# Key-weight squares on another engine, four heads' scores in one PSUM bank, and a new table of wanted times in a decoder kernel

## The chip, the cores and the metric

The kernel runs on one core of a Trainium2 chip. The core has a matrix engine (PE, TensorE), a vector engine (DVE), a scalar engine (ACT), a general engine (POOL, GpSimd) and a queue that issues its DMA transfers (SP). Each engine works through its own list of instructions in the order in which the program wrote them; semaphores make it wait for others. The metric is the device time of one execution in microseconds. Before the change it is 1154.83 us, the median of three runs (1154.33 to 1157.21).

## The reference

The input `x` holds 16 sequences of 256 rows of 512 numbers, the context `ctx_2048` as many. Three layers are added to the stream, each after a layer norm:

```
x = x + attn(layernorm(x))            # 16 heads of 32, causal, softmax
x = x + xattn(ctx, ctx, layernorm(x)) # long convolution of key-value products, times the query
x = x + ffn(layernorm(x))             # 512 -> 2 x 1408 -> 512, silu(gate) * up, int8-style rounding
```

For attention, `q`, `k` and `v` are `x @ w.T + b`; the scores of a head are `q @ k.T / sqrt(32)`, masked above the diagonal; softmax; times `v`; then `@ o_w.T + o_b`. The second layer multiplies every pair of 8 channels of a head of the context, convolves along the sequence with a kernel per head, multiplies by the normed stream and sums. The third rounds the input rows and the weights to 255 levels with a scale per row, forms gate and up, rounds their product again per row, and multiplies by the down weights.

## The kernel before

**Attention.** A unit is one sequence and one group of four heads: 64 units. The projections split every fp32 operand into a high and a low fp16 half and add three products (`mm3`). The halves need a power-of-two scale for each weight matrix. For that `proj_norm` (line 599) squares each of the four weight matrices, 512 x 512 numbers laid out as 128 partitions of 2048, with one ACT instruction (line 603) whose accumulator gives the sum of squares of each partition in a column of `top`; the squared matrix itself is written to a tile that is overwritten later. `scale_bound` (line 608, DVE) joins two columns with the biases' squares, `scale_turn` (613, PE), `scale_top` (618 to 621, DVE), `scale_diag` (625, ACT), `scale_spread` (629, PE) and `scale_all` (634 on, DVE) turn the columns into one scale, first for the query and key weights, later for the value and output weights. `proj_hi` (657, ACT) and `proj_lo` (662, DVE) then write the halves that the first projection (667 to 669, PE) needs. Beside this the first sequences are normed (688 to 699 on DVE, 694 on POOL, 705 and 714 on ACT, 721 on POOL) and turned by DMA (727).

The projected queries and keys of a unit are split (775 on ACT, 780 on DVE), stored and read back stacked (787, 795). `scores_mm` (line 800) then makes the scores: for the first 128 queries (`qc` 0) against 128 keys and for the last 128 (`qc` 1) against 256, two heads to one tile `s` of `[128, 2, 256]` fp32, which is one PSUM bank; at `qc` 0 half of each bank is not used. A unit so takes four such tiles, out of two buffers. `scores_max` (line 815) adds the mask and takes the row minimum of the negated scores, one DVE instruction per head (line 819, with an accumulator read into `nmax`); `scores_exp` (826, ACT) follows, then transposes (851, PE) and their copies (859, 861), the weighting by `v` (879 to 886, PE; 892 to 904), and the output projection (`pj_o`), whose rows are added at line 754 and stored at 759. Alongside POOL and ACT form the context's products (930 to 974) and the feed-forward weights are rounded (1043 to 1069).

**Convolution and feed-forward.** A tile is 16 positions of 8 sequences: 32 tiles. `conv_mm` (324 to 326, PE) multiplies by shifted taps, `conv_mul` (338 to 344, DVE) by the query, `conv_sum` (352 to 368, POOL or DVE as `sum_on` says) adds up eight terms, lines 374 and 380 bring the result back. `gate_mm` (425, PE) makes gate and up in four column groups each, `gate_scale` (432, DVE), `gate_silu` (436, ACT), `gate_ups` (443), `up_mul` (450), `up_top` (454) and `up_round` (472) follow, `down_mm` (510, PE), `down_scale` (519, DVE; for tiles 28 to 30 517, ACT) and `down_rows` (528, DVE; for those tiles 524 and 525, POOL) end a tile. Three PSUM buffers serve gates, ups and down products together.

**The order of the work.** No loop writes the program. Each step is given to a planner (`Plan`, line 35) with a key, an engine, a wanted time (`when`), a duration, the steps it comes after, and the buffers it takes (`new`) and uses. `order` (line 63) walks through time; whenever an engine is free it picks, of the steps that are ready and whose buffers are free by the planner's own durations, the one with the smallest wanted time. What it picks becomes the order of instructions on that engine. Before this, every wanted time is moved by an entry of the table `shift` (line 1371), one row for each kind of step, one of eight columns by the stretch of time in which the step lies (`bounds`, line 1370). The chip then runs the fixed lists, and waits where a thing isn't ready.

The kinds that matter below: `pn` squares of a weight matrix, `xc` shift of a sequence's norm, `sm` and `sx` scores and their minimum, `qm` projection, `cm` convolution matmuls, `cs` convolution sums, `gm` gate and up matmuls, `dm` down product, `ds` and `dr` the last two steps of a tile.

Of the kernel before, what the change touches and what calls it, by code (L numbers as in the profile page):

```python
# [8 lines left out]
F32 = mybir.dt.float32  # L9
# [5 lines left out]
ALU = mybir.AluOpType  # L15
# [93 lines left out]
def kernel(  # L109
# [433 lines left out]
    if True:  # L543
# [55 lines left out]
        def proj_norm(nm):  # L599
            j = names.index(nm)  # L600
            pool = wp if nm == "o" else wqp
            hi = pool.tile([P, KC, D], F16, name=f"w{nm}_hi")
            nc.scalar.activation(hi, wraw[nm], AF.Square, accum_out=top[:, j:j + 1])
            wT[nm] = hi, pool.tile([P, KC, D], F16, name=f"w{nm}_lo")
# [195 lines left out]
        def scores_mm(b, g, qc, h2):  # L800
# [6 lines left out]
            stk, nk = stks[b, g], P * (qc + 1)  # L807
            ps = ps_s.tile([P, 2, S], F32, tag="s", name=f"s{b}_{g}_{qc}_{h2}")
            for hh in range(2):
                nc.tensor.matmul(  # L810
                    ps[:, hh, :nk], stk[:, 2 * h2 + hh, 0, qc * P:(qc + 1) * P], stk[:, 2 * h2 + hh, 1, :nk],
                    start=True, stop=True)
            pss[b, g, qc, h2] = ps

        def scores_max(b, g, qc, h2):
            ps, nk = pss.pop((b, g, qc, h2)), P * (qc + 1)
            for hh in range(2):
                h = 2 * h2 + hh
                nc.vector.tensor_tensor_reduce(  # L819
                    out=prs[b, g][qc][:, h, :], in0=ps[:, hh, :nk], in1=mask2[:, P - qc * P:2 * P],  # L820
                    op0=ALU.add, op1=ALU.min, scale=esc[:, 0:1], scalar=BIG,
                    accum_out=prs[b, g][2][:, qc, h:h + 1])
# [268 lines left out]
        for n, nm in enumerate(names):  # L1091
# [3 lines left out]
            pl.add(("pn", nm), "ACT", w, 1.9, proj_norm, nm, late=0.2, after=[("pi", nm)], then=[("ph", "k", 3)] * (nm == "o"))  # L1095
# [23 lines left out]
        def unit(i):  # L1119
# [18 lines left out]
            if True:  # L1138
                p = t - 1.3 * T
                for n in range(4):  # L1140
                    qc, h2 = divmod(n, 2)
                    s = ("s", (i, n))
                    pl.add(("sm", i, n), "PE", p + 1.2 * n, 0.22, scores_mm, b, g, qc, h2, late=0.2,
                           after=[("qt", i, m) for m in range(5)] + [("sm", i, n - 1)] * (n > 0), new=[s] + [("pr", i)] * (n == 0),
                           use=[s, ("st", i)])
                    pl.add(("sx", i, n), "DVE", p + 1.2 * n + 0.5, 0.55 + 0.26 * qc, scores_max, b, g, qc, h2, late=0.15,
                           after=[("sm", i, n)], use=[s, ("pr", i)])
# [145 lines left out]
        for i in range(NT):  # L1293
# [78 lines left out]
            ("bi", 2): (10.4, 0.3, -0.3, 11.6, -6.5, -5.6, 1.1, 9.7),  # L1372
            ("bk", 3): (14, 19.5, 6, 6, -10.4, -13.9, 10.4, -14.9),
            ("bn", 2): (15.7, -13.2, -4.1, -1, 3.3, 9.8, -19, 4.7),
            ("bp", 2): (-4.5, -4, 7.8, 7.5, 5.5, 7.9, -10.4, 0.1),
            ("bq", 2): (8.9, -2.5, -4.8, 14.6, -19.3, 5.7, 4.6, -2.5),
            ("br", 2): (-11.6, 0.1, -1.8, 25.7, -11.6, 30.3, -20.9, 27.1),
            ("bs", 2): (-0.5, 4.8, 18.6, 12.2, 20.4, 5.3, 10.4, 14.8),
            ("bt", 2): (-0.6, -1.7, 13.7, 1, 17.6, 5.9, 5.3, 14.1),
            ("ck", 2): (-1.3, -31.7, -19.1, -1, -11.9, -0.7, 7.9, 0.4),  # L1380
            ("cl", 3): (0.6, -7.7, -12, -2.3, -3.8, -7.7, -12.3, 2.5),
            ("cm", 2): (-9, -2.3, -2.3, -2.3, 19.8, -10.3, -1.9, 4.4),
            ("cm", 3): (10.3, -22.2, -22, 2.3, 9.7, 3.6, 13, -6.2),
            ("co", 2): (-0.4, -22.8, 0.2, 5.5, 6.5, 3.8, -22.9, -30.5),
            ("cr", 2): (-15, 0.1, -6.1, -1.1, 1.9, -10, -1.5, 2),
            ("cs", 3): (-19, -8.1, -43, -11.5, -16.3, -7.1, -35.8, -43.3),
            ("ct", 3): (-9.4, -11.9, -11.9, -10.2, -14.9, -1.2, -20.9, -2.8),
            ("cu", 3): (15.8, -0.8, 16.3, 15.7, -6.4, -1.8, -5.6, -6.1),
            ("cw", 2): (4.6, 16.4, 9.8, 8.6, 1.4, 8.9, 16.5, 8.9),
            ("cx", 2): (2.9, -0.4, 0.6, 4.4, -23.3, 2.7, -8.6, 4.1),  # L1390
            ("cz", 2): (2.1, -2.4, 2.1, 0.1, -6.6, 0.8, 2.8, 6.1),
            ("dm", 2): (5.8, 5.8, 2.8, 9.7, 3.1, 9.1, 48.5, 52),
            ("do", 2): (-8.3, -10.7, -10.7, -16.2, -1.5, -4.8, -5.9, -2.9),
            ("dr", 2): (3.4, -0.9, -5.3, -4.7, 1, 0.8, 0.8, 1),
            ("ds", 2): (15, 26.3, 26.2, 14.1, 15, 1.2, 1.2, 25.1),
            ("fc", 3): (-0.1, -1.9, -33.2, -0.2, -38.2, 0, 1.5, -0.1),
            ("fd", 2): (-5.7, 1, 1.9, 9, -7.9, 7.3, 8, 7.5),
            ("fm", 2): (-54, 5.4, 2.9, -0.1, -1.3, 2.9, -48.2, 2.9),
            ("fm", 3): (0.7, -1.4, -0.4, 9.3, -3.2, -0.4, -15.7, 8.2),
            ("fn", 2): (4.3, 0.8, 0, 0.8, 0.8, 2.2, -8.7, -5.2),  # L1400
            ("fo", 2): (-32, -13, -0.6, -18.7, -3.9, -21.4, -14.1, -2.4),
            ("fp", 2): (-47.6, -7.9, -5.9, -45.1, -52.6, -2.5, -5.9, -47.7),
            ("fq", 2): (-2.1, -4.4, 9.4, 9.4, -4, 7.5, -1.9, 17.2),
            ("fr", 2): (14.5, -22.4, 13.7, 5.7, 0.1, 15.1, -26.4, -7.3),
            ("fs", 2): (-9.9, -0.4, -7.8, -0.2, 0.3, 1.2, -16.3, -6.7),
            ("ft", 2): (-4.5, -2.9, -4.1, 8.7, 1.5, 11.4, -3.8, -2.2),
            ("fv", 2): (10.5, -0.2, -0.4, -7.5, -7, 7, 5.3, -3.1),
            ("fw", 2): (-6.5, -2.2, -23.6, -2.5, -24.4, 47.6, -2.2, -28.3),
            ("gl", 3): (-0.8, 4.7, 1.7, -0.8, -1.6, 9.1, -0.7, -3.7),
            ("gm", 4): (-1.6, -8.8, -14.6, 0.6, -6.3, -12.5, -11.6, -1.6),  # L1410
            ("gs", 3): (9.6, 5.1, 9.9, 20.7, 9.6, 13.9, 9.6, 10),
            ("gu", 3): (6.9, 10.9, -1.3, 7.4, -1.3, 14, -1, -7),
            ("om", 4): (7.7, 14.8, 13.4, -6, 11.9, -12.4, -6.9, -3),
            ("or", 3): (3.8, 9.6, -0.5, 16.5, 8.2, 3.1, 1.7, 3.2),
            ("os", 3): (0.3, 0.3, -7.2, 2.8, 0.6, -0.9, -1, -1.2),
            ("pa", 2): (-0.3, 3.8, 5.3, 13, 8.9, -1.8, 9.2, 5),
            ("pb", 2): (6.7, -0, -18.4, -2.1, 1.1, 1.1, 4, -21.6),
            ("pc", 2): (-1, -1, 1.2, -9.2, 1.6, 2.5, -1, -9.1),
            ("pd", 2): (-1.4, -0.6, -0.7, -10.8, 3.2, -10.2, -8.9, -10.2),
            ("pe", 2): (-5.8, 1, 10.8, -1.9, 0.1, -1.9, -6.2, -6.2),  # L1420
            ("pf", 2): (-13, -24.8, -17, -1.9, -25.9, -24.3, -28.3, -10.4),
            ("pg", 2): (6.9, 8.4, -0.4, 0.2, -5.6, 6.9, 8.6, 8.1),
            ("ph", 2): (12.6, -10.9, 5, -1.1, 16.4, 19.2, -1.1, -0.5),
            ("ph", 3): (-17.2, -0, -0.6, -5.1, 1.8, 1.8, 1.8, 1.8),
            ("pi", 2): (8, -1.4, 3, -3.4, -11.8, -4.2, 3.3, 1.5),
            ("pl", 2): (-0.8, 7, 56.1, 39.7, 3.7, -0.8, 3.8, -0.8),
            ("pl", 3): (0.8, -0.1, -2.9, 1.5, -0.1, -20.6, -4.6, -1.5),
            ("pm", 2): (13.7, -20.3, 13.7, 1.9, 5, 3.7, 3.5, 11),
            ("pm", 3): (21.8, 5.6, 14.3, 14.2, -34.9, -22.3, -45.6, 0.6),
            ("pn", 2): (7.4, -4.5, -2.2, -2, -2.3, -6, 1.6, -2.3),  # L1430
            ("ps", 2): (-0.3, 0.4, 2.2, 1.7, -13.3, 2.2, 0.2, 0.1),
            ("qh", 3): (-57, -52.8, -25.6, 3.6, -52.3, 9, 9.2, -53.8),
            ("ql", 3): (0.7, -25.8, -3.7, -21.2, -28.1, -0.1, -20.4, -8),
            ("qm", 3): (1.3, -8.8, 3.3, 1.9, -3.8, 1.3, 1.3, 5.1),
            ("qs", 2): (-22.4, -18, -16.2, -5.9, -20.9, -8.2, -5.8, -9.6),
            ("qt", 3): (-5.2, -9.7, 1.2, 21.2, 1.3, -7.6, -0.7, -10.5),
            ("se", 3): (-16, 18.3, 14, 16.5, -5.8, 25.4, 16.4, 20.1),
            ("si", 2): (0.4, -14.7, -6.1, 4.3, -1.4, 3.3, -15.6, -7.5),
            ("sl", 2): (0.1, 7.8, 0.1, 6, -5.4, -2.8, -10.9, -6),
            ("sm", 3): (5.3, -1, -0.3, 3.5, -3.5, 3.8, -1, -3.6),  # L1440
            ("sx", 3): (-16.8, -2.9, -15.5, 1.1, 0.1, -15.4, 0.1, 1.1),
            ("tk", 2): (-2.5, -4.7, 2.4, -26.7, -36.7, -7.3, -4.7, 3.4),
            ("ub", 3): (0.7, 14.1, 11, 0, -4.6, -0.4, -0.1, -1.6),
            ("ud", 3): (-2.5, -0.8, 5.8, 2.2, -4.5, -12, -0.8, 5.1),
            ("uf", 3): (2, -5.5, 5.8, -16.6, -2.9, -0.3, -0.3, 7.8),
            ("ui", 2): (5.4, 0.3, -0.4, 6.2, -9.5, -8.5, -30.5, 4.9),
            ("um", 3): (2.3, 3.8, 3.8, 3.5, 3, 4.9, -2, -2.4),
# [66 lines left out]
```

## Time and profile before

| | us |
|---|---|
| median of three runs | 1154.83 (1154.33 to 1157.21) |
| the profiled execution's own time | 1159.2 |
| its span, first to last instruction | 1157.4 |
| PE busy | 1078.9 (93%) |
| DVE busy | 1007.9 (87%) |
| POOL busy | 950.0 (82%) |
| ACT busy | 839.1 (72%) |

The profile is of one execution, recorded instruction by instruction. It took 4.4 us more than the median of the runs, so what is worked out from it is set against its own time first. Busy is the time in which an engine had an instruction in work; matmuls overlap, so a busy PE may still be short of its best rate. A line of the timeline gives the start, the time, the engine, the line of the program, the operation, what it writes and reads, and, in brackets, how long the engine had stood idle and what ended that. The clock is the share of PE's full clock that was granted. Attention fills the span up to about 600 us, the convolution and the feed-forward part the rest; the last tile's chain ends at 1157.

### The profile page before, as it was taken

To read this page: it belongs to the slowest core of one execution; us is meant where nothing else is said; L and a number is where in the kernel's file an instruction comes from. 1 tells how busy PE (TensorE), PEld (TensorE's weight loads), DVE (VectorE), ACT (ScalarE), POOL (GpSimd) and SP (SyncE) were. 2 spreads that over 40 slices of the span, in tenths; PEclk is the share of its full clock that TensorE was granted. 3 is DMA by queue.
4 is the path that set the end of the run, shared out by engine and by line. 5 is a ranking of instruction groups with operands and counts; after the bars stand their busy time and mean duration, and the time that the engine had idled before them with its cause. 6 is when DMAs were issued, how large, how long until landed. Compare 5 with 4: busy or idle time off the path is not lost.

```text
span 1157.4 us, 25647 instructions
## 1 busy us (share of the span) xinstructions
PE 1078.9 (93%) x8503; PEld 764.3 (66%) x8503; DVE 1007.9 (87%) x3184; ACT 839.1 (72%) x2005; POOL 950.0 (82%) x924
## 2 busy tenths in 40 slices
PE   3998999999999999999999889999999999999966
PEld 3675667576766767676766566676777776666632
DVE  4998777989888899797687999998999999999996
ACT  6898789999989989899784456574656656665444
POOL 4398999999798983888545789999999999999952
PEclk9999999999999999999999999999999999999988
DMA  8587978799697787887468746766676786666322
GB/s 281 163 179 225 280 243 224 230 269 263 189 260 242 235 233 195 230 244 211 169 229 293 238 133 177 185 161 163 183 188 164 183 187 176 167 168 179 78 53 61
DMA packets 236259, 229.48 MB, mean 198 GB/s; under 512 B 125177, under 2 KB 182559, under 8 KB 235999
## 3 DMA queue, kind: packets, MB, share of 16 engines
q1 hardware_dynamic: 236127, 227.85, 70.3%
q8 instruction: 67, 1.10, 0.4%
q14 instruction: 65, 0.53, 0.1%
HBM read 124.10 MB, written 75.74 MB: 173 GB/s over the span
## 4 chain that ended last, share of the span: by engine, by line
PE 45%; DVE 20%; POOL 16%; ACT 7%; DMA 5%; issue 5%; SPq 1%; POOLq 0%; DVEq 0%; ACTq 0%
PE g L425 6%; PE c L324 3%; PE c L326 3%; PE c L325 3%; DVE p L819 3%; POOL g L443 3%; PE d L510 3%; PE pj_qk L667 3%; PE pj_qk L669 2%; PE pj_qk L668 2%; PE pt L851 2%; POOL u L357 2%; ACT p L826 2%; PE s L810 2%; DVE qkhl L780 2%
## 5 line engine op out<-in xcount | busy, mean ns | idle before, releaser
L826 ACT ACTIVATE p<-p,nmax 128x256 f32<-128x256 f32 (+1 forms) x512 | 231.1, 455 | 6.6 <-DVE nmax L819 5.6
L819 DVE CUSTOM_DVE_ANT_0 p<-s,mask,esc 128x128 f32<-128x128 f32 (+1 forms) x512 | 187.4, 410 | 23.5 <-PE s L810 22.7
L324 PE MATMUL c<-bkv,T 128*128 128x288 f16 x640 | 183.4, 287 | 6.7 <-issue 3.9
L425 PE MATMUL g<-w,xq 128*128 128x384 bf16 (+1 forms) x1024 | 172.2, 319 | 13.6 <-DVE o L528 6.3
L326 PE MATMUL c<-bkv,T 128*128 128x288 f16 x640 | 183.5, 287 | 0.0
L325 PE MATMUL c<-bkv,T 128*128 128x288 f16 x640 | 183.5, 287 | 0.0
L974 POOL TENSOR_TENSOR kv<-p,kv 128x1152 f16<-128x1152 f32 x64 | 152.5, 2384 | 7.5 <-ACT kv L969 7.4
L425 PEld LDWEIGHTS <-xq 128*128 128x128 bf16 x1024 | 101.3, 100 | 70.5 <-issue 12.4
L956 POOL TENSOR_TENSOR p<-kT 128x1024 f32<-128x1024 f32 x64 | 144.0, 2250 | 2.9
L443 POOL TENSOR_TENSOR g<-g,sw 128x704 f32<-128x704 f32 x60 | 101.1, 1707 | 4.5 <-ACT g L436 4.4
L826 ACT ACTIVATION_READ_ACCUMULATOR p<-p,nmax 128x1 f32 x512 | 101.0, 197 | 0.0
L810 PE MATMUL s<-st 96*128 96x128 f16 (+1 forms) x512 | 84.9, 247 | 8.0 <-DVE nmax L819 7.8
L338 DVE TENSOR_TENSOR u<-c,qT 128x512 f32<-128x512 f32 x128 | 87.2, 681 | 5.8 <-PE c L326 5.5
L510 PE MATMUL d<-w,hq 128*128 128x512 bf16 x352 | 82.7, 384 | 3.8 <-DVE hp L450 3.0
L780 DVE SCALAR_TENSOR_TENSOR qkhl<-pj_qk,bias,qkhl 128x256 f16<-128x256 f32 x128 | 60.4, 476 | 29.3 <-ACT qkhl L775 11.8
L775 ACT ACTIVATE qkhl<-pj_qk,bias 128x256 f16<-128x256 f32 x128 | 60.0, 471 | 33.7 <-PE pj_qk L669 21.1
L357 POOL TENSOR_TENSOR u<-u 128x512 f32<-128x512 f32 x60 | 77.7, 1294 | 5.9 <-DVE u L338 5.9
L969 ACT CAST kv<-p 128x1152 f16<-128x1152 f32 x64 | 73.6, 1149 | 11.4 <-DMA kv_d<-kv 10.6
L851 PE MATMUL pt<-idf,p 128*128 128x128 f32 x512 | 77.5, 274 | 2.1 <-ACT kT L943 1.9
L324 PEld LDWEIGHTS <-T 128*128 128x128 f16 x640 | 62.7, 98 | 25.0 <-issue 4.5
L667 PE MATMUL pj_qk<-xhT,wk_hi 128*128 128x256 f16 x256 | 69.7, 272 | 7.4 <-ACT qkhl L775 3.8
L325 PEld LDWEIGHTS <-T 128*128 128x128 f16 x640 | 62.7, 98 | 16.8
(236 smaller groups left out, 3273.8 us busy)
## 6 DMA issues: line engine op xcount, KB each, us to landing
kv_d<-kv SPq DMA_DIRECT2D x64, 576.0 KB, 3.5
bkv<-kv_d SPq DMA_DIRECT2D x64, 576.0 KB, 3.9
qk_d<-qkhl SPq DMA_DIRECT2D x64, 256.0 KB, 2.7
st<-qk_d SPq DMA_DIRECT2D x256, 64.0 KB, 2.7
T<-pad_d SPq DMA_DIRECT2D x64, 256.0 KB, 4.4
x_d<-xt SPq DMA_DIRECT2D x32, 256.5 KB, 3.1
bx<-x_d SPq DMA_DIRECT2D x32, 256.5 KB, 3.5
xt<-in_x_dram SPq DMA_DIRECT2D x16, 512.0 KB, 5.1
```

What stands on the lines that cost most here:

```text
L324: nc.tensor.matmul(reg, T[:, 0, d:d + P], kv[:, mi, 0, :], start=mi == 0, stop=False)
L325: nc.tensor.matmul(reg, T[:, 0, d:d + P], kv[:, mi, 1, :], start=False, stop=False)
L326: nc.tensor.matmul(reg, T[:, 1, d:d + P], kv[:, mi, 0, :], start=False, stop=mi == li)
L425: nc.tensor.matmul(pg[:, :c.stop - c.start].rearrange("p (r o) -> p r o", o=P), t["xq"][:, kc, :], w1[:, (o + c.start) // P:(o + c.stop) / ...
L443: (nc.gpsimd if i < NT - 2 else nc.vector).tensor_tensor(ts[i]["g1"][:, c], ts[i]["g1"][:, c], sw1[:, I + c.start:I + c.stop], ALU.mult)
L510: nc.tensor.matmul(pd.rearrange("p (r o) -> p r o", o=P), t["hq"][:, ic, :], w2[:, :, ic, :], start=ic == 0, stop=ic == IC - 1)
L667: nc.tensor.matmul(ps, lh, rh, start=first, stop=False)
L810: nc.tensor.matmul(ps[:, hh, :nk], stk[:, 2 * h2 + hh, 0, qc * P:(qc + 1) * P], stk[:, 2 * h2 + hh, 1, :nk], start=True, stop=True)
L819: nc.vector.tensor_tensor_reduce(out=prs[b, g][qc][:, h, :], in0=ps[:, hh, :nk], in1=mask2[:, P - qc * P:2 * P], op0=ALU.add, op1=ALU.min, ...
L826: nc.scalar.activation(pr[:, h, :], pr[:, h, :], AF.Exp, scale=-1.0, bias=nmax[:, qc, h:h + 1], accum_out=lsum[:, qc, h:h + 1])
L956: nc.gpsimd.tensor_tensor(ap(p, 0, [[NKV, 4], [64, 4], [1, 64]]), ap(kT, o, [[96, 4], [0, 4], [1, 64]]), ap(kT, o, [[96, 4], [8, 4], [1, 6 ...
L974: nc.gpsimd.tensor_tensor(kv[:, :, 1, :], p, kv[:, :, 0, :], ALU.subtract)
```

## The change

Three things change.

The squares of the key weights leave ACT. DVE takes mean and variance of each of the four blocks of 512 numbers of a partition, joins them, forms mean squared plus variance, and multiplies by 2048. The other three matrices stay on ACT. The step is given to the planner as 2.9 us on DVE instead of 1.9 us on ACT.

The scores of the first 128 queries of all four heads go into one bank, as four blocks of 128 columns; the scores of the last 128 queries stay two heads to a bank. A unit so takes three tiles `s`, not four. The matmuls and reductions are the same in number and shape, and the reductions still come in two steps of two heads, both from the one tile; its step on PE is planned at 0.24 us.

All 100 rows of the table `shift` have other numbers. Of these the diff below shows the ones that the prediction speaks of.

```diff
@@ proj_norm
-            nc.scalar.activation(hi, wraw[nm], AF.Square, accum_out=top[:, j:j + 1])
+            if nm == "k":
+                st, mv = wld.tile([P, KC, 6], F32, name="wst"), wld.tile([P, 2], F32, name="wmv")
+                for o in range(KC):
+                    nc.vector.bn_stats(st[:, o, :], wraw[nm][:, o, :])
+                nc.vector.bn_aggr(mv, st)
+                nc.vector.scalar_tensor_tensor(top[:, j:j + 1], mv[:, 0:1], mv[:, 0:1], mv[:, 1:2], ALU.mult, ALU.add)
+                nc.vector.tensor_scalar(top[:, j:j + 1], top[:, j:j + 1], float(KC * D), None, ALU.mult)
+            else:
+                nc.scalar.activation(hi, wraw[nm], AF.Square, accum_out=top[:, j:j + 1])
@@ scores_mm
-            stk, nk = stks[b, g], P * (qc + 1)
-            ps = ps_s.tile([P, 2, S], F32, tag="s", name=f"s{b}_{g}_{qc}_{h2}")
-            for hh in range(2):
+            stk, nk, nh = stks[b, g], P * (qc + 1), 4 - 2 * qc
+            ps = ps_s.tile([P, 2 * S], F32, tag="s", name=f"s{b}_{g}_{qc}_{h2}").rearrange("p (h k) -> p h k", h=nh)
+            for hh in range(nh):
                 nc.tensor.matmul(
-                    ps[:, hh, :nk], stk[:, 2 * h2 + hh, 0, qc * P:(qc + 1) * P], stk[:, 2 * h2 + hh, 1, :nk],
+                    ps[:, hh, :], stk[:, 2 * h2 + hh, 0, qc * P:(qc + 1) * P], stk[:, 2 * h2 + hh, 1, :nk],
                     start=True, stop=True)
-            pss[b, g, qc, h2] = ps
+            pss[b, g, qc, h2] = ps[:, 0:2, :]
+            if qc == 0:
+                pss[b, g, 0, 1] = ps[:, 2:4, :]
@@ the steps
-            pl.add(("pn", nm), "ACT", w, 1.9, proj_norm, nm, late=0.2, after=[("pi", nm)], then=[("ph", "k", 3)] * (nm == "o"))
+            pl.add(("pn", nm), "DVE" if nm == "k" else "ACT", w, 2.9 if nm == "k" else 1.9, proj_norm, nm, late=0.2, after=[("pi", nm)], then=[("ph", "k", 3)] * (nm == "o"))
...
-                    s = ("s", (i, n))
-                    pl.add(("sm", i, n), "PE", p + 1.2 * n, 0.22, scores_mm, b, g, qc, h2, late=0.2,
-                           after=[("qt", i, m) for m in range(5)] + [("sm", i, n - 1)] * (n > 0), new=[s] + [("pr", i)] * (n == 0),
-                           use=[s, ("st", i)])
+                    m = n if qc else 0
+                    s = ("s", (i, m))
+                    if n != 1:
+                        pl.add(("sm", i, n), "PE", p + 1.2 * n, 0.24, scores_mm, b, g, qc, h2, late=0.2,
+                               after=[("qt", i, k) for k in range(5)] + [("sm", i, max(0, n - 1 - (n == 2)))] * (n > 0), new=[s] + [("pr", i)] * (n == 0),
+                               use=[s, ("st", i)])
                     pl.add(("sx", i, n), "DVE", p + 1.2 * n + 0.5, 0.55 + 0.26 * qc, scores_max, b, g, qc, h2, late=0.15,
-                           after=[("sm", i, n)], use=[s, ("pr", i)])
+                           after=[("sm", i, m)], use=[s, ("pr", i)])
@@ shift
-            ("cm", 3): (10.3, -22.2, -22, 2.3, 9.7, 3.6, 13, -6.2),
-            ("cs", 3): (-19, -8.1, -43, -11.5, -16.3, -7.1, -35.8, -43.3),
-            ("dr", 2): (3.4, -0.9, -5.3, -4.7, 1, 0.8, 0.8, 1),
-            ("ds", 2): (15, 26.3, 26.2, 14.1, 15, 1.2, 1.2, 25.1),
-            ("gm", 4): (-1.6, -8.8, -14.6, 0.6, -6.3, -12.5, -11.6, -1.6),
-            ("pn", 2): (7.4, -4.5, -2.2, -2, -2.3, -6, 1.6, -2.3),
-            ("xc", 2): (17.2, 42, 5.9, -5.1, 10.4, 2.7, 17.2, -0.6),
+            ("cm", 3): (-3.5, 5.5, 7.5, 3.6, 15.1, 0.9, 8.2, -2.2),
+            ("cs", 3): (-12.9, -10, -12.9, 3.7, -29.7, -41.9, 0.5, -15.2),
+            ("dr", 2): (-25.1, -17.7, -0.7, 2.7, -0.7, 2.7, 6.5, -4.8),
+            ("ds", 2): (22.5, 5.4, 11.8, 8, 9.3, 8, 22.6, 14),
+            ("gm", 4): (-12.5, 5.3, -2.7, 9.1, 1.7, 5.7, -2.9, 9.4),
+            ("pn", 2): (7.9, 1.2, -0, 0.6, -0.7, -11.5, 0.6, -13.8),
+            ("xc", 2): (-8.7, 12.2, -19.4, 0.9, 2.3, -6.6, -1.6, -27.9),
...
```

## The prediction

> **What bounds the kernel now.** I read the head of the page first, then the busy time by stage, then what PE waits for, then the timeline of the two places where the change can be followed instruction by instruction: the first 23 us and the last 50.
>
> The page says that PE is the busiest engine and that its clock is granted in full except in the last two slices.
>
> ```profile
> span 1157.4 us, 25647 instructions
> PE 1078.9 (93%) x8503; PEld 764.3 (66%) x8503; DVE 1007.9 (87%) x3184; ACT 839.1 (72%) x2005; POOL 950.0 (82%) x924
> PEclk9999999999999999999999999999999999999988
> ```
>
> An average of 93% hides where the other 7% lies. The busy time by stretch of the span shows it (columns: stretch, its length, busy us and instructions of each engine, granted clock, DMA share, GB/s). The reader subtracts PE's busy time from the length: 18.5 us idle in the start, 26.4 in the attention part, 10.4 where attention hands over to the convolution, 2.0 in the long body of convolution and feed-forward, 21.7 in the tail, and in two pieces of the tail a clock of 0.63 after a stretch in which PE did nearly nothing.
>
> ```profile
> 0.00:40.00 40.00, 21.48 (x153) 17.59 (x154) 21.72 (x77) 24.63 (x37) 14.35 (x19) 1.00 0.73 230
> 40.00:600.00 560.00, 533.56 (x4658) 384.81 (x4656) 471.12 (x1824) 499.52 (x1513) 465.51 (x375) 1.00 0.80 226
> 600.00:720.00 120.00, 109.62 (x807) 77.20 (x806) 108.16 (x281) 65.01 (x120) 86.00 (x102) 0.97 0.72 224
> 720.00:1096.00 376.00, 373.95 (x2684) 264.09 (x2682) 357.13 (x903) 220.50 (x301) 356.07 (x403) 1.00 0.65 168
> 1096.00:1158.00 62.00, 40.27 (x210) 20.65 (x207) 49.74 (x104) 29.40 (x37) 28.08 (x28) 0.89 0.25 53
> 1108.00:1115.00 7.00, 0.98 (x6) 0.37 (x5) 6.86 (x8) 0.72 (x2) 6.84 (x6) 0.88 0.09 19
> 1115.00:1122.00 7.00, 7.00 (x33) 4.08 (x32) 5.47 (x13) 1.70 (x2) 2.81 (x3) 0.63 0.14 37
> ```
>
> So PE's own work bounds all but the ends: any order of the same instructions can win only out of these 79 us, and 376 us of the body offer nothing. PE's list of waits names the two largest that the change can reach (columns: total us, times, longest).
>
> ```profile
> PE s L810 <- DVE nmax L819: 7.8, 9, 2.8
> PE g L425 <- DVE o L528: 6.3, 2, 6.0
> ```
>
> **The key weights' squares.** Removed: one ACTIVATE of 1.906 us and its accumulator read of 0.187 us on ACT. Added on DVE: four BATCH_NORM_STATS2 (the row of 512 elements is 0.686 us), one aggregate (0.182), one scalar_tensor_tensor (about 0.22, the two of line 608 are 0.15 and 0.28), one tensor_scalar (0.154): 4 x 0.686 + 0.182 + 0.22 + 0.154 = 3.30 us. The timeline of before shows the chain that it sits in:
>
> ```profile
> 12.83 0.34 DVE L699 TENSOR_SCALAR mv_a<-mv_a,r_a 128x1 f32<-128x1 f32 x2 [0.81 <-POOL r_a L694]
> 13.01 1.91 ACT L603 ACTIVATE wk_hi<-wl_k 128x2048 f16<-128x2048 f32 x1
> 15.04 0.28 DVE L608 SCALAR_TENSOR_TENSOR top<-top,tbp 128x2 f32<-128x2 f32 x1 [1.88 <-ACT wk_hi L603]
> 16.06 1.89 ACT L603 ACTIVATE wv_hi<-wl_v 128x2048 f16<-128x2048 f32 x1
> 17.95 0.28 ACT L625 ACTIVATE t<-idf,t 2x2 f32<-2x2 f32 x1
> 22.36 0.42 PE L667 MATMUL pj_qk<-xhT,wq_hi 128*128 128x256 f16 x1
> ```
>
> The key weights were issued at 3.34 and landed 9.6 later, at 12.94. DVE can start there and ends at 16.24, where ACT ended at 15.01: line 608 comes 1.2 us later. But line 608 was not what ACT's line 625 waited for. From 15.04 to the end of line 621 passed 1.37 us, so the number was ready at 16.41, and ACT took the value weights' square first (16.06 to 17.95). After the change that number is ready at 16.3 + 1.4 = 17.7, and ACT, free of the key square since 13.1, takes the value weights when they land (3.89 + 11.8 = 15.7) and is done at 15.7 + 1.89 + 0.19 = 17.8. Line 625 then starts at 17.8, against 17.95. Bounds: 1.5 earlier if ACT does not take the value square first and DVE is quicker than its rows, 1.2 later if nothing of the wait is absorbed. I take 0. Behind the new wait for the key weights on DVE is queued the shift of batch 1 (line 699, wanted at -24.8 now, the squares at -66.1): about 3.4 us later, and with it batch 1's rows on ACT, its split on POOL and its two transposes on SP. Their user is the projection of unit 4, wanted 35 us after that of unit 0; that cover costs nothing, and without it the price is 3.4 us.
>
> **Scores of four heads in one bank.** PE's matmuls stay 512 (8 for each of 64 units), with the same shapes, and so do DVE's 512 reductions: no busy time goes. What changes is the ring of two score banks: a unit takes three of them, not four, and the first is held for four reductions instead of two. PE waited 7.8 us for such a bank, in 9 of 256 groups, all in the attention part where PE is the bound. Bounds: -7.8, all of it gone; +7.8, as much again, because the third tile now waits for four reductions in the same bank (0.27 us from one to the next of the 128-wide form in the timeline). With a quarter of the requests gone and one of the remaining three in each unit held longer, I take half of the wait away: -4. Late next, where it goes, is the same engine at its next wait: PE's projections wait 8.2 us for the split of qkhl on DVE and ACT (4.4 and 3.8).
>
> The Trainium skill speaks against this part: "Perfetto Trace Analysis", Optimizing Tensor Performance, Matmuls, says that independent matmul groups should rotate through different PSUM banks, so that one bank is read out while the next is filled. By that rule the two head pairs no longer overlap, and two more reductions, 0.54 us, would stand before a score matmul of each of 64 units: an estimate of +35 us, a sum near 1188. No run here shows it; in the trace of before PE stood idle for only 9 of 256 groups, so I do not sum by it.
>
> **Wanted times anew.** Every step's wanted time moves, so all five queues get another order, SP's some 880 DMA issues and POOL's 924 instructions among them. No instruction is added, so this is bounded by stage. Attention: its stretch from 120 to 240 us has PE busy 111.63 of 120 (7.0% idle), that from 360 to 480 117.46 (2.1%). Over 560 us these give 39 and 12 us idle, against 26.4: between +12.7 and -14.5. Nothing I can read in the table says which, so 0. Handover: between -8 and +8 (its 10.4 us gone to the body's rate, or nearly doubled). The convolution's loads still stand ahead of the large weight loads in SP's queue: 0. Body: PE 99.5%, POOL 95% of its stretch; a POOL order that lets the convolution's sums run late would first use POOL's 20 us of slack; 0, at worst +2, the idle there doubled.
>
> The tail can be followed. The last convolution, the second head of tile 31, is wanted at 1064.0 - 6.2 = 1057.8 before and 1061.8 after; the four up groups of tile 28 at 1053.8 to 1058.3 before and from 1064.8 after. So three groups, 12 matmuls of 0.163 us (12 in 1.95), go behind that convolution, whose chain of sums, norm, gates and down product ends the kernel: it starts 2.0 us earlier against the same remaining PE work. I take -2. The other thing to see there is a stall:
>
> ```profile
> 1104.77 2.54 PE L510 MATMUL d<-w,hq 128*128 128x512 bf16 x11
> 1107.18 1.89 DVE L368 TENSOR_TENSOR oT<-u,vsum 128x256 f32<-128x256 f32 x1
> 1109.10 1.87 DVE L362 TENSOR_TENSOR vsum<-u 128x352 f32<-128x352 f32 x1
> 1111.01 1.47 DVE L363 TENSOR_TENSOR vsum<-vsum,u 128x352 f32<-128x352 f32 x1
> 1113.87 0.69 DVE L528 TENSOR_TENSOR o<-d,x 128x512 f32<-128x512 f32 x1
> 1114.62 6.99 PE L425 MATMUL g<-w,xq 128*128 128x384 bf16 x28 [6.01 <-DVE o L528]
> ```
>
> A down product is done at 1107.2, but DVE works through 5.9 us of the last tile's sums before it frees the bank; PE stands 6.0 us, and its next 28 matmuls take 0.250 us each, not 0.163: 2.4 us more. Eleven down products at 1130 take 4.15 us instead of 2.37 after a 2.8 us wait: 1.8 more. Together 10.2 us. The sums are still wanted ahead of that release (1057.3 against 1072.5, before 1029.2 against 1083.6), so whether the stall returns hangs on when both are ready: -10.2 if it goes, +10.2 if it comes twice, 0 taken.
>
> **The sum.** 0 (start) - 4 (score banks) - 2 (tail) = -6. The profiled execution took 1159.2 us (span 1157.4 and 1.8 around it), 4.4 above the median of the three runs, 1154.83. So 1153.2 for that execution, and 1148.8 on the median: I predict 1149.
>
> **The rivals.**
> - *The freed wait is given back* (PE goes on to the next wait, the qkhl split, and the tail stays as it is): 1152 to 1158. For it: PE is busy 95% of the attention part and the wait to come is as large as the one that goes. Against: 18.6 us of other idle time remain there.
> - *The tail's stall comes twice* (slower): DVE again takes 6 us of sums while PE's next bank waits, and a second such burst, from the wide reductions of line 454 (1.6 us) or the gates' scale, catches PE too. +10.2 - 4 = about +6: 1161. It decides as soon as more than 4 us are lost there. For it: DVE is 80% busy in the tail and the sums keep their place ahead of the release. Against: the sums are wanted 28 us later than before.
> - *The attention part takes the rate of its worst stretch* (slower): +12.7 - 2 for the tail, with no gain from the banks: 1165. For it: the stretch exists in this trace. Against: the same engines reach 2.1% idle in another.
> - *The order also heals the attention part* (faster): down to the best stretch's rate, -14.5 in which the score wait is contained, and -2: 1138.
>
> **How the numbers follow.** Forecast 1149, own range 1145 (the score wait wholly gone) to 1151 (about half of both terms): 0.36; the healed attention part, 1136 to 1144: 0.14; given back: 0.15; the tail's stall twice: 0.19; worst stretch: 0.16. A measurement of this kernel tells about 0.3%, 3.5 us, from no change; so faster (below 1151.3) 0.50, same 0.15, slower (above 1158.3) 0.35. The range leaves out about one in ten at each side: 1139, short of the healed case's end, and 1165, the worst stretch's middle.
>
> **What the profile after would show.** Line 603 three times on ACT and four statistics on DVE near 13 us, the first projection within 0.5 us of 22.36. PE's wait for nmax under 4 us in all; over 8 says the held bank costs. PE idle in 40 to 600 us between 12 and 39, and the body still near 2. In the tail PE's wait for line 528, and whether a clock of 0.63 stands behind it. The prediction is wrong if the new order moves PE's idle time of the attention part or of the tail by more than the terms above: they are the least known.

## The result and the profile after

The changed kernel takes 1150.49 us, the median of six runs (1148.86 to 1157.87). The kernel before has a median of 1157.78 over six runs, the three named ahead of the prediction among them. The ratio of the two is 0.9948, with a 95% interval from 0.9924 to 0.9972: about 6 us less. A later set of runs gave 1148.74 against 1158.10, 0.9924 [0.9909, 0.9939]. The profiled execution of the changed kernel took 1151.33 us, that of before 1159.2. Single executions of either kernel mostly lie within 3 us of its median, a few up to 7 off, so a small difference of a stage between two profiles is worth little; where it matters a second profile of the same kernel is set beside the first. The diff moves line numbers: 608 is now 616, 625 is 633, 667 is 675, 699 is 707, 775 and 780 are 783 and 788, 810 and 819 are 818 and 829; up to 599 they stay.

The head of the page of the changed kernel: PE has 6.6 us less busy time for the same 8503 matmuls, ACT 6.8 us less; the seven new DVE instructions do not show in DVE's sum. PE's sum is no saving of the change: it is 1075.8 in a second profile of the changed kernel, and 1073.4 in a profile of the order of before (`old_order_dve`, below).

```profile
span 1149.5 us, 25640 instructions
PE 1072.3 (93%) x8503; PEld 765.1 (67%) x8503; DVE 1008.1 (88%) x3191; ACT 832.3 (72%) x2003; POOL 948.3 (83%) x924
PEclk9999999999999999999999999999999999999989
```

Its busy time by the same five stretches (stretch, length, busy us and instructions of PE, weight loads, DVE, ACT and POOL, granted clock, DMA share, GB/s):

```profile
0.00:40.00 40.00, 20.50 (x140) 17.13 (x141) 24.25 (x86) 22.62 (x34) 14.12 (x19) 1.00 0.72 227
40.00:600.00 560.00, 535.73 (x4684) 387.27 (x4681) 471.64 (x1832) 499.60 (x1520) 465.36 (x375) 1.00 0.78 228
600.00:720.00 120.00, 110.69 (x835) 79.47 (x834) 108.97 (x278) 62.28 (x115) 90.56 (x108) 0.99 0.75 224
720.00:1096.00 376.00, 371.76 (x2669) 263.53 (x2668) 359.75 (x913) 224.53 (x306) 356.06 (x404) 1.00 0.63 168
1096.00:1158.00 62.00, 33.62 (x185) 17.71 (x183) 43.50 (x88) 23.32 (x31) 22.23 (x20) 0.91 0.23 50
```

PE's idle time is 19.5 us in the start (18.5 before), 24.3 in attention (26.4), 9.3 in the handover (10.4) and 4.2 in the body (2.0). No stage stands out; the second profile of the changed kernel has 23.1 in attention and 2.8 in the body, and that of `old_order_dve`, which has the order of before and its time within 0.2%, has 23.3 in attention, 10.8 in the handover and 3.2 in the body. So the differences in attention and body do not repeat, and the handover's is 1 us. PE's waits for DVE and ACT that the prediction followed (total us, times, longest):

```profile
PE pj_qk L675 <- ACT qkhl L783: 7.8, 11, 1.4
PE g L425 <- DVE o L528: 6.3, 2, 6.0
PE s L818 <- DVE nmax L829: 5.7, 10, 1.5
...
PE pj_qk L675 <- DVE qkhl L788: 1.5, 5, 0.7
```

The wait of the score matmuls for their bank fell from 7.8 to 5.7 us (in the profile of `old_order_dve` it is 6.8). In the same trace the projections' wait for ACT's half of the split rose from 3.8 to 7.8, and that for DVE's half fell from 4.4 to 1.5. The three together were 16.0 us and are 15.0. The stall of the tail stands where it stood, 6.0 us long.

The start (start us, duration, engine, line, operation, and in brackets the idle time before it and what ended it):

```profile
12.95 2.47 DVE L606 BATCH_NORM_STATS2 wst<-wl_k 128x6 f32<-128x512 f32 x4 [1.24 <-DMA wl_k<-in_L_attn_k_w_dram]
15.65 1.91 ACT L611 ACTIVATE wv_hi<-wl_v 128x2048 f16<-128x2048 f32 x1 [2.90 <-DMA wl_v<-in_L_attn_v_w_dram]
16.08 0.33 DVE L707 TENSOR_SCALAR mv_a<-mv_a,r_a 128x1 f32<-128x1 f32 x2
16.32 0.15 DVE L616 SCALAR_TENSOR_TENSOR top<-top,tbp 128x2 f32<-128x2 f32 x1
17.60 0.29 ACT L633 ACTIVATE t<-idf,t 2x2 f32<-2x2 f32 x1
17.80 1.50 ACT L713 ACTIVATE xn<-xt,mv_a,r_a 128x512 f32<-128x512 f32 x2
20.29 0.68 ACT L665 ACTIVATE wq_hi<-wq,sc 128x512 f16<-128x512 f32 x1
22.73 0.42 PE L675 MATMUL pj_qk<-xhT,wq_hi 128*128 128x256 f16 x1
```

DVE is done with the squares at 16.16, 3.2 us after it starts. The chain through line 633 is 0.35 us ahead of before. Then ACT norms both rows of the next sequence (line 713, 1.50 us, and line 722 behind it, to 20.38) ahead of the weights' high half. Before, one of the two rows had been done at 15.34, ahead of the value weights' square, and only the other, 0.80 us, came here. So the first projection comes at 22.73, 0.37 us later than before.

### The profile page after: what moved, and what is told of

The parts are those of the page before. It is cut to its first block, busy times and chain, and to the rows that moved or that the text cites. A ratio compares the mean times of both kernels' runs of the same rounds, so it can differ in the third digit from the quotient of the medians.

```text
span 1149.5 us, 25640 instructions
## 1 busy us (share of the span) xinstructions
PE 1072.3 (93%) x8503; PEld 765.1 (67%) x8503; DVE 1008.1 (88%) x3191; ACT 832.3 (72%) x2003; POOL 948.3 (83%) x924
## 4 chain that ended last, share of the span: by engine, by line
PE 32%; DVE 11%; POOL 4%; DMA 2%; issue 2%; ACT 1%; SPq 0%; DVEq 0%; POOLq 0%; ACTq 0%
PE g L425 8%; PE c L324 5%; PE c L326 4%; PE c L325 4%; PE d L510 4%; DVE hp L450 2%; DVE s L454 1%; DVE u L338 1%; DMA T<-pad_d 1%; POOL g L443 1%; DVE u L341 1%; DVE oT L368 1%; DVE g L432 1%; PE sd_o L374 1%; POOL u L357 1%
## 5 line engine op out<-in xcount | busy, mean ns | idle before, releaser
L836 ACT ACTIVATE p<-p,nmax 128x128 f32<-128x128 f32 (+1 forms) x512 | 230.6, 454 | 3.9 <-DVE nmax L829 3.6
L285 ACT ACTIVATE xn<-x,rn_f 128x512 f32<-128x512 f32 x32 | 26.0, 813 | 82.9 <-DVE rn_f L280 82.9
L979 ACT CAST kv<-p 128x1152 f16<-128x1152 f32 x64 | 73.5, 1149 | 10.6 <-DMA kv_d<-kv 6.4
L818 PE MATMUL s<-st 96*128 96x128 f16 (+1 forms) x512 | 74.3, 247 | 5.8 <-DVE nmax L829 5.7
L324 PEld LDWEIGHTS <-T 128*128 128x128 f16 x640 | 62.6, 98 | 25.5 <-issue 4.8
```

What stands on the lines that cost most here:

```text
L324: nc.tensor.matmul(reg, T[:, 0, d:d + P], kv[:, mi, 0, :], start=mi == 0, stop=False)
L836: nc.scalar.activation(pr[:, h, :], pr[:, h, :], AF.Exp, scale=-1.0, bias=nmax[:, qc, h:h + 1], accum_out=lsum[:, qc, h:h + 1])
```

## The experiments

Four theories were on record. **1**: the four-head bank pays by itself, 2 to 4 us. **2**: only the new order pays, in the run-in of the convolution (**2a**) or in the attention part (**2b**). **3**: the table is worth something only with the steps that it was made for. All ratios are to the kernel before, run on the same chip in the same set.

### The bank without the order, and the order without the bank

`old_order_bank4` keeps the table and steps of before, and with them every engine's order. The first of the two score steps makes all four heads' scores in one bank, the second issues nothing.

```diff
         def scores_mm(b, g, qc, h2):
...
+            if (qc, h2) == (0, 1):
+                return
...
+            stk, nk, nh = stks[b, g], P * (qc + 1), 4 - 2 * qc
...
```

> The order of before, only that the four heads' first scores go into one bank at the first of the two steps. Theory 1 (the bank pays: PE waits less for DVE): 2 to 4 us under before, PE's wait for nmax from 7.8 to under 5 us. Theory 2 (only the new order pays): within 1 us of before, the wait for nmax may fall but comes back at the next wait of the attention part.

`new_order_pairs` is the changed kernel in its own order, but with two heads to a bank again: the one score step takes both buffers.

```diff
...
-            ps = ps_s.tile([P, 2 * S], F32, tag="s", ...).rearrange("p (h k) -> p h k", h=nh)
...
+            for h3 in ((0, 1) if qc == 0 else (h2,)):
+                ps = ps_s.tile([P, 2, S], F32, tag="s", name=f"s{b}_{g}_{qc}_{h3}")
...
```

> The changed kernel's order, but each pair of heads in a bank of its own again, so that the first score step needs both buffers. Theory 1: 2 to 4 us over the changed kernel, that is 2 to 4 under before, with a wait for nmax of 8 us or more. Theory 2: as the changed kernel, about 6 under before. If the new order leans on the bank more than the old one did, it is slower than before by 5 us or more.

Measured: 0.9992 [0.9982, 1.0002] for the bank alone, 1155.72 against 1156.67 us; 1.0149 [1.0129, 1.0169] for the order without it, 1172.36 us. PE's waits in the old order with the one bank:

```profile
PE g L425 <- DVE o L528: 6.3, 2, 6.0
PE av L883 <- DVE al L908: 5.3, 4, 3.7
...
PE s L812 <- DVE nmax L823: 3.4, 5, 1.0
```

and in the new order with pairs apart, its first wait and its attention stretch:

```profile
PE s L819 <- DVE nmax L828: 33.0, 38, 2.9
```

```profile
40.00:600.00 560.00, 515.17 (x4512) 373.92 (x4510) 459.42 (x1763) 485.28 (x1460) 460.53 (x370) 1.00 0.76 220
```

In the unchanged order the bank takes 4.4 us off its own wait, 7.8 to 3.4, and no gain can be measured: by the interval it is between 2.1 us less and 0.2 more. Of the 4.4 us 2.5 are back in one place, PE's wait for DVE's `al` (line 908 in that kernel), 5.3 us where before had 2.8. The attention stretch, with the one bank and then with pairs apart in the same order (`old_order_dve`), shows PE as busy either way (in the execution that was profiled before the change it was 533.56):

```profile
40.00:600.00 560.00, 536.47 (x4700) 388.45 (x4698) 474.97 (x1846) 502.71 (x1527) 465.51 (x376) 1.00 0.79 229
```

```profile
40.00:600.00 560.00, 536.73 (x4685) 387.43 (x4685) 474.08 (x1840) 502.40 (x1522) 466.50 (x375) 1.00 0.78 229
```

In the new order the bank matters: without it the kernel is 22 us slower, and PE waits 33.0 us for banks, 38 times. This version asks for both buffers at one place of PE's list, so it shows that the new order relies on the one bank, not what pairs apart would cost in an order made for them. So the packing is not a term of its own. Theory 1 falls.

### The table and the steps, each alone

`old_table_new_code` has both code changes and their steps with the table of before; `new_table_alone` is the kernel before with the new table.

```diff
         shift = {
-            ("cm", 3): (-3.5, 5.5, 7.5, 3.6, 15.1, 0.9, 8.2, -2.2),
+            ("cm", 3): (10.3, -22.2, -22, 2.3, 9.7, 3.6, 13, -6.2),
...
```

> Both code changes and their steps, with the table of before. Theory 1: 2 to 4 us under before. Theory 2 (the gain is in the wanted times): not under before; the lead of 4 us that the changed kernel wins between 640 and 770 us is missing.

> The code and steps of before with the changed table. Theory 3 (a table is worth something only with the steps it was made for): over before by 10 us or more, with PE waiting for nmax 15 us or more. If the table is better by itself: 2 to 6 us under before.

Measured: 1.0075 [1.0063, 1.0088], 1165.65 us, for the new code with the old table; 1194.95 us in the one run of the old code with the new table, beside 1158.1. The four corners, as ratios to before:

| | table of before | new table |
|---|---|---|
| code and steps of before | 1 | 1.032 (one run) |
| new code and steps | 1.0075 | 0.9948, again 0.9924 |

Neither half helps, both together do: theory 3 holds. The steps alone make another order, since the planner fills the place of a step that is gone or has moved to another engine; that order is 9 us slower, while the bank's code in the old order costs nothing. What a badly fitting table does is seen in PE's waits of the old code with the new table:

```profile
PE sd_pt L851 <- ACT kT L943: 25.6, 1, 25.6
PE s L810 <- DVE nmax L819: 14.0, 24, 3.0
```

One wait of 25.6 us is as long as two thirds of the 37 us that this run takes more. The wait for nmax, expected at 15 us or more, is 14.0 and not the largest loss.

### Which columns of the table

The table's first five columns hold up to wanted time 570, about the attention part, the last three the rest. `hyb_early_new` takes the first five from the new table and three from the old, `hyb_late_new` the other way round, both with the new code.

```diff
# hyb_early_new, one row of 100, against the changed kernel
-            ("cm", 3): (-3.5, 5.5, 7.5, 3.6, 15.1, 0.9, 8.2, -2.2),
+            ("cm", 3): (-3.5, 5.5, 7.5, 3.6, 15.1, 3.6, 13, -6.2),
# hyb_late_new, the same row
-            ("cm", 3): (-3.5, 5.5, 7.5, 3.6, 15.1, 0.9, 8.2, -2.2),
+            ("cm", 3): (10.3, -22.2, -22, 2.3, 9.7, 0.9, 8.2, -2.2),
```

> Both code changes; of the table the columns up to wanted time 570 as changed, the later three as before. Theory 2a (the gain of the table lies in the run-in of the convolution, 640 to 770 us): 0 to 2 us under before. Theory 2b (it lies in the attention part): 4 to 6 under before, as the changed kernel.

> Both code changes; the columns up to 570 as before, the later three as changed. Theory 2a: 4 us better than both code changes with the whole old table, so 4 to 5 us over before. Theory 2b: 8 to 9 over before, as with the whole old table.

Measured: 0.9976 [0.9965, 0.9988], 1154.3 us, and 1.0064 [1.0051, 1.0076], 1164.32 us. In us that is 2.8 under before and 7.4 over; each lies between the ranges of the two theories. From the old table in the new code (1.0075) the early columns take 0.0099, 11.5 us; the late ones 0.0011 on the old early ones and, by the changed kernel's two results, 0.0028 or 0.0052 on the new, 3 or 6 us (the intervals overlap for the first and not for the second). Theory 2b names the larger part. Where it lies, two windows show. The new code with the old table:

```profile
60.00:80.00 20.00, 13.95 (x108) 9.13 (x101) 14.83 (x64) 14.49 (x42) 15.99 (x15) 0.83 0.46 132
100.00:120.00 20.00, 16.28 (x101) 11.19 (x99) 15.64 (x66) 16.46 (x54) 16.66 (x14) 0.74 0.49 172
```

The changed kernel:

```profile
60.00:80.00 20.00, 16.86 (x138) 12.09 (x137) 17.60 (x72) 16.75 (x49) 17.51 (x18) 0.91 0.65 155
100.00:120.00 20.00, 18.25 (x163) 12.44 (x162) 17.35 (x55) 16.62 (x49) 18.40 (x16) 1.00 0.78 251
```

In these 40 us PE is busy 30.23 us with the old table and 35.11 with the new, and does 209 matmuls instead of 301. The two longest waits in the old-table windows:

```profile
70.90 0.69 PE L889 MATMUL av<-idf,lb 128*128 128x128 f32 x2 [3.91 <-DVE nmax L829]
...
107.34 1.11 PE L861 MATMUL pt<-idf,p 128*128 128x128 f32 x4 [2.94 <-ACT t L869]
```

Up to 152 us PE has done 925 matmuls with the old table, 936 with the late columns alone, and 1017 to 1025 in the two profiles of the changed kernel and that of the early columns alone. Up to 600 us the gap to the old table is 70 to 90, no larger, and from 152 to 600 us PE is busy 432.6 us with the old table and 432.4 in the changed kernel. At 560 us for some 4700 matmuls, 0.12 us each, 90 of them are 11 us: nearly the whole gain of the early columns is made in the first 152 us of the kernel. Against the kernel before, which had done 1001, the changed kernel leads by some 20, about 2 us: most of that gain only undoes what the new steps broke. Counts of matmuls of different orders compare roughly, since the shapes differ.

The late columns' 3 to 6 us do not show as the idle time of one stage. The count says 600 to 720 (835 matmuls against 800 with the early columns alone), but the second profile of the changed kernel has 813 there. Between which points they are made can be read from DVE's 384 products of the convolution (lines 338 to 344): the first starts at 611.9 and 610.6 us in the two profiles of the changed kernel and at 610.8 with the early columns alone, the last at 1095.1, 1094.0 and 1098.0. So by these traces some 4 us are made between the end of attention and the tail. Theory 2a, which names 640 to 770 us, is left open for this smaller part.

### The key squares on one engine or the other

`new_order_act` gives the squares back to ACT in the changed kernel's order; `old_order_dve` gives them to DVE in the order of before. The planner's steps stay as they are in both.

```diff
# new_order_act, in proj_norm
-            if nm == "k":
-                st, mv = wld.tile([P, KC, 6], F32, name="wst"), wld.tile([P, 2], F32, name="wmv")
...
-            else:
-                nc.scalar.activation(hi, wraw[nm], AF.Square, accum_out=top[:, j:j + 1])
+            nc.scalar.activation(hi, wraw[nm], AF.Square, accum_out=top[:, j:j + 1])
```

> The changed kernel in its own order, only that ACT squares the key weights. My working of the start: the value weights' square on ACT covers the difference, so within 1 us of the changed kernel and the first projection within 0.5 us. Rival (the squares on DVE hold up the start): 1 to 2 us under the changed kernel.

> The kernel of before in its own order, only that DVE squares the key weights. By my working within 1 us of before. Rival: line 608 comes 1.2 us later and nothing covers it, 1 to 2 us over before.

Measured: 0.9928 [0.9913, 0.9942] with ACT in the new order, where the changed kernel itself gave 0.9948 and 0.9924; 1.0008 [0.9996, 1.0019] with DVE in the old order. In neither order can a difference of the engine be measured, but the intervals are too wide to exclude the rivals' 1 to 2 us. In the new order the first projection comes at 22.82 with ACT and 22.73 with DVE. The old order with DVE shows the start when the cover is gone:

```profile
17.18 1.89 ACT L611 ACTIVATE wv_hi<-wl_v 128x2048 f16<-128x2048 f32 x1
...
19.07 0.28 ACT L633 ACTIVATE t<-idf,t 2x2 f32<-2x2 f32 x1
...
23.48 0.42 PE L675 MATMUL pj_qk<-xhT,wq_hi 128*128 128x256 f16 x1
```

There ACT's list has a row of the next norm first. It waits for the shift that DVE now does behind the squares, starts at 16.46, and the value weights' square follows at 17.18. So the first projection comes 1.1 us later than before. The measured time is 0.9 us over before, with an interval from 0.5 under to 2.2 over, which neither shows nor excludes those 1.1.

### The tail

`tail_release_first` is the changed kernel with DVE's last two steps of tile 27, which free the PSUM buffer, put ahead of the last tile's sums.

```diff
-            for s in pl.order():
+            seq = pl.order()
+            early = [s for s in seq if s["key"] in (("ds", 27), ("dr", 27))]
+            seq = [s for s in seq if s not in early]
+            at = next(n for n, s in enumerate(seq) if s["key"] == ("cs", 62, 2))
...
+            seq[at:at] = early
+            for s in seq:
```

> The changed kernel, only that DVE's last two steps of tile 27 come ahead of the last tile's sums. If the stall of 6 us in the tail and the slow matmuls behind it are on the path that sets the end, as I priced them: 6 to 8 us under the changed kernel, 12 to 14 under before. Rival: the last tile's own chain sets the end whatever PE does: 0 to 2 under the changed kernel, or 1.4 over it, the two steps' own time on DVE.

Measured: 0.9906 [0.9893, 0.9919], 1145.96 us, the best time of all runs. The tail of the changed kernel:

```profile
1098.49 2.54 PE L510 MATMUL d<-w,hq 128*128 128x512 bf16 x11
1100.87 1.46 PE L425 MATMUL g<-w,xq 128*128 128x384 bf16 x8
1108.34 5.72 PE L425 MATMUL g<-w,xq 128*128 128x384 bf16 x24 [6.01 <-DVE o L528]
...
1115.15 0.60 PE L374 MATMUL sd_o<-idf,oT 128*128 128x128 f32 x4
```

and with the release first:

```profile
1096.02 2.54 PE L510 MATMUL d<-w,hq 128*128 128x512 bf16 x11
1098.39 1.46 PE L425 MATMUL g<-w,xq 128*128 128x384 bf16 x8
1100.13 0.82 PE L425 MATMUL g<-w,xq 128*128 128x384 bf16 x4 [0.28 <-DVE o L528]
1105.62 4.27 PE L425 MATMUL g<-w,xq 128*128 128x256 bf16 x20 [4.66 <-DVE hp L450]
...
1111.14 0.60 PE L374 MATMUL sd_o<-idf,oT 128*128 128x128 f32 x4
```

The 6.01 us are gone, and PE stands 4.66 us four matmuls later: the next buffer is freed by line 450, on DVE, behind the same sums. From the start of the down product to the transposes of the last convolution's result it takes 15.12 us instead of 16.66, and to the end of the span 49.5 instead of 51.0. The busy time of the stretch, in the changed kernel, with the release first, and in `act_tail2`, which comes next (columns as above):

```profile
1098.49:1115.15 16.66, 10.21 (x49) 5.32 (x47) 14.78 (x25) 4.54 (x5) 12.72 (x11) 0.80 0.16 39
```

```profile
1096.02:1111.14 15.12, 9.58 (x50) 5.04 (x48) 13.87 (x25) 4.55 (x5) 12.61 (x11) 0.89 0.18 43
```

```profile
1094.90:1110.25 15.35, 10.74 (x49) 5.29 (x47) 13.86 (x25) 5.13 (x6) 12.75 (x12) 0.84 0.17 43
```

Two more versions, made on `new_order_act`, go at that wait too. `act_tail2` also puts the multiplications of line 450 for tile 28 ahead of the last sums; `act_tail3` besides delays the row maximum of tile 29 (line 454), with what hangs on it, behind the multiplications of tile 30. The changed kernel was run again beside them.

```diff
...
+            later([("cs", 62, 2)], ("dr", 27))       # act_tail2, act_tail3
+            later([("cs", 63, 1)], ("um", 28, 3))    # act_tail2, act_tail3
+            later([("ut", 29, 0)], ("um", 30, 3))    # act_tail3
...
```

(`later` puts a step, and what hangs on it, behind another.)

> The changed order with ACT squaring the key weights; in the tail DVE takes the last steps of tile 27 before the sums of tile 31, and the four up products of tile 28 before the second of those sums. If PE's wait for banks in the tail is the path: the 4.7 us wait that stayed when only tile 27 went ahead falls under 3 us, and the time lies 2 to 3 us under that run, near 1143, with 1 to 2 us more from ACT if the squares on DVE cost that: 11 to 15 under before. Rival (the last tile's chain sets the end, and is now held up): as with tile 27 alone or slower.

> The same, and the row maximum of tile 29 goes behind the last tile's and the up products of tile 30, for which PE's last wait of 2.8 us stands. If that wait is on the path: 2 to 3 us under the run without it. Rival: tile 29 is late for its own down product: same or up to 2 us over it.

> The changed kernel itself, beside the others of this set: 5 to 7 us under before.

Measured, in one set: 0.9913 [0.9898, 0.9929] for `act_tail2`, 0.9921 [0.9906, 0.9936] for `act_tail3`, 0.9924 [0.9909, 0.9939] for the changed kernel itself. The 11 to 15 us under before that were expected of `act_tail2` did not come; it is 10 under. Nor did the further 2 to 3 that were named for `act_tail3`. In `act_tail2` PE's wait for line 450 falls to pieces of at most 1.5 us, PE waits 2.20 us for line 432 instead, and the stretch to the transposes takes 15.35 us, no less than with the release alone:

```profile
1101.35 4.25 PE L425 MATMUL g<-w,xq 128*128 128x256 bf16 x16 [1.51 <-DVE hp L450]
1107.80 0.60 PE L425 MATMUL g<-w,xq 128*128 128x256 bf16 x4 [2.20 <-DVE g L432]
1109.02 1.44 PE L425 MATMUL g<-w,xq 128*128 128x384 bf16 x4 [0.62 <-DVE g L432]
```

Each time the wait moves to another of DVE's instructions. In `act_tail3` PE's wait of 2.8 us at line 510 falls to 1.55, and PE stands 3.20 us for line 406 (`xq`) next. In the stretch DVE stands idle for 1.2 to 1.9 us in each of the three traces, so its own work is most of what the stretch takes, and an order mainly chooses whom PE waits for. The release first is worth 1.5 us of the stretch by its trace; 0.9 of them are DVE's 25 instructions there taking 13.87 us instead of 14.78, the two sums at lines 362 and 363 above all (2.40 us instead of 3.34), and why these differ wasn't tried. By its ratio it is ahead of the changed kernel's two results by 0.0018, with intervals that overlap, and by 0.0042, with intervals that just don't, all in different sets. It beats the kernel before by 0.9%; by how much it beats the changed kernel isn't settled.

## Why the prediction came out as it did

The sum was -6 us and the measured ratio is worth -6.0 [-8.8, -3.2]; the forecast of 1149 stands against 1150.49, inside the range of 1145 to 1151. It was counted from 1154.83, the median of the first three runs of before; from the median of all six, 1157.78, the same sum would have given 1151.8. The terms behind it did less well than their sum.

- **Start, 0: right.** The squares take 3.21 us on DVE (3.30 worked out), the line that was 625 starts at 17.60 (17.8 worked out) and the first projection is 0.37 us late, inside the 0.5. The shift of batch 1 is pushed back 3.25 us as foreseen; in the new order no cost of it can be seen, in the old one it puts the first projection 1.1 us back. What the working missed is that ACT now takes both rows of the next norm ahead of the weights' high half; the new order does so with the squares on ACT too. Both single-engine runs agree with the zero, to within some 2 us.
- **Score banks, -4: wrong as a term.** The step that failed is "half of the wait goes, so the time goes". The nmax wait did not come under 4 us as forecast; it is 5.7, and 4.9 in the second profile. In the old order it did come down, to 3.4, and the time did not follow: the wait for `al` grew by 2.5 us, and PE was as busy as with pairs apart. This is the rival "the freed wait is given back", and the place named as late next, the split of `qkhl` on ACT, is where it went in the new order. What the prediction didn't see at all is that the new order would rely on the bank, and be 22 us slower without it.
- **The rule against one bank.** The Trainium skill, "Perfetto Trace Analysis", Optimizing Tensor Performance, Matmuls, has independent matmul groups rotate through different PSUM banks. The estimate by it was +35 us; measured in an unchanged order is 0.9992, and going back to separate banks in the new order costs 1.0149. So the price that was worked out from the rule does not show here. That with two buffers fewer requests count for more than overlap between the halves of one would fit, but wasn't tried by itself.
- **Attention, 0 within -14.5 and +12.7: the bounds held, the reason was incomplete.** They were meant for the table. The steps alone make an order that is 0.75% slower, 9 us, and the table's early columns take 11.5 off; what is left against before is small. The prediction treated the steps' own effect on the order as nothing. The rivals of a healed attention part and of its worst rate are both outside what happened: 24.3 us idle, near the old 26.4.
- **Handover and body, 0: nearly right.** -1.1 us and +2.2 us of PE idle in the first profile (+0.8 in the second), the body's bound having been +2. The second figure is within what two profiles of one order differ by (2.0 and 3.2 in that of before). Of the late columns' 3 to 6 us some 4 are made here by the traces, and the prediction had no term for them.
- **Tail, -2: wrong.** It was read from the wanted times alone that the last convolution would move ahead of twelve matmuls of tile 28. PE's order over its last 61 planner steps is the same in both kernels, and the last convolution stands ahead of those twelve matmuls in both. A wanted time only ranks the steps that are ready with their buffers free; here readiness and buffers decided. From the down product before the stall to the end of the span the profile of before has 52.6 us and that after 51.0, but the second profile of the changed kernel has 52.4 in the same order, so this isn't the change's doing.
- **The stall of the tail, 0 of +-10.2: right to take nothing, wrong in its price.** It neither went nor doubled. The part of the price that the release first removes, 6.0 us and the slow matmuls' 2.4, gave 1.5 us of the stretch, or 2 to 5 by the ratios: the price took PE's stall and slow clock as time on the path, while DVE was busy for all but 1.9 us of the stretch. The last term of the price, 1.8, also sets the length of a row, 4.15, against a time from start to start, 2.37; from start to start both, it is 1.6.

So the total was right partly by luck: a gain of 4 that isn't a gain by itself and one of 2 that did not happen stood in for two pieces of the table that could not be read from it, 2.8 us from new steps and early columns together and 3 to 6 from the late ones. Why the late columns gain is open.

## What to carry to other kernels

When an order comes from a planner, its table of wanted times, its steps and its buffers are one thing: here new steps without their table, the table without its steps and the order without its bank cost 0.8 to 3%, where together they gained half a percent; so price them together, and expect that a step that leaves a queue also moves what stood behind it. A wait that disappears from PE's list is worth only what the next late engine leaves of it; before pricing a stall, look whether the engine that ends it is itself busy without a gap, because then moving its work mostly moves the stall. Compare one stage of two profiles only beside a second profile of the same kernel.

## What was not expected of the hardware

**The clock after a wait.** In the two windows of the attention part that hold the old table's longest waits (3.91 and 2.94 us) the granted clock was 0.83 and 0.74; the changed kernel had 0.91 around a wait of 3.0 us and 1.00 where its longest wait was 1.5. Over 152 us the clock was 0.94 against 0.99. PE was busy 6.2 us less there (117.60 against 123.78), while the 92 matmuls that it was behind are some 11 us by the estimate above, so the waits seem to have cost more than their own length. That the wait causes the lower clock wasn't tried by itself, and the same order also varies: from 60 to 80 us `act_tail2` and `act_tail3`, which differ only in the tail, both have a wait of 3.0 us, and clocks of 0.91 and 0.83.

**The same order at two speeds.** Eleven down matmuls of tile 28 behind the same wait of 2.79 us took 2.53 us in the first profile of the changed kernel and 4.22 in the second:

```profile
1123.87 2.53 PE L510 MATMUL d<-w,hq 128*128 128x512 bf16 x11 [2.79 <-DVE hp L450]
```

```profile
1122.76 4.22 PE L510 MATMUL d<-w,hq 128*128 128x512 bf16 x11 [2.79 <-DVE hp L450]
```

So 1.7 us of the tail differ from execution to execution with nothing changed in the program, more than the 1.5 us that the release first gains in its stretch.
